# Weights of three later layers prepared in slices during the first layer and kept in DRAM

## The chip, the core and the metric

The kernel runs on one core of a Trainium2 chip. The metric is the device time of one execution in microseconds (us). All data are 32-bit floats. The engines are called as in the profile: PE (TensorE, matrix products; PEld is its loading of the stationary operand), DVE (VectorE), ACT (ScalarE), POOL (GpSimd) and SP (SyncE, which here issues nearly all DMAs). SBUF is the on-chip memory of 128 partitions, PSUM the eight banks into which PE writes, DRAM the memory off the core.

## What is computed

The input x has 128 batch elements of 128 nodes by 512 features, and adj one 128 x 128 matrix for each element. Four graph layers follow one another, and each ends with `x = layernorm(x + layer(x, adj))`:

- Layer 0: a transition matrix T is made from adj and from scores of the nodes; the result is `relu(x Wk0 + T x Wk1 + T T x Wk2 + biases)`.
- Layer 1: two hypergraph convolutions. The first multiplies by w1 (1024 x 512, used transposed), a layer norm with gamma and beta follows, the second multiplies by w2 (512 x 1024, transposed).
- Layer 2: an attention by scores `x w a`, then a product with w (512 x 512).
- Layer 3: eight-headed attention with wq, wk, wv and wo (512 x 512 each, transposed).

Before a layer can run, its weights must be brought into the form that its products read: w1, w2, wq, wk, wv and wo have to be transposed, gamma is multiplied into w2, and some vectors (beta through w2, bv through wo, w times a) are worked out.

## The kernel before

**Tiling.** Two batch elements make a pair (U = 2). There are n = 64 pairs, and one group of work is two pairs; each layer thus has 32 groups. The functions `layer0` (line 894), `layer1` (1007) and `layer23` (1168, layers 2 and 3 together) write down one group's work. Between layers x goes through DRAM (`x1d`, `x2d`).

**Products by Strassen's scheme.** `strassen` (565) makes a product of two 2 x 2 block matrices by seven products, with the weight blocks B11, B21, T1, B22, T2, T3 and N4, where T1 = B12 - B11, T2 = B22 - T1, T3 = B22 - B12 and N4 = B21 - T2 (`combine`, 493). `twice` (761) does this on two levels: seven outer products in the order B11, B21, T2, T1, B22, T3, N4, each of them a `strassen` of seven: 49 products on 49 inner blocks. The weights of layer 0, w1 and the pair wq with wk are used by `twice`; w2, w, wv and wo by one level.

**Preparation.** `load_T` (500) loads 128 rows of a weight at a time, transposes each 128 x 128 part on PE against an identity matrix into PSUM (`ident`), copies it to SBUF on ACT and at the end subtracts blocks on DVE. With `by_blocks` it first regroups the columns on DVE. `prepare1` (972) does this for w1 and w2, `prepare2` (1122) for wq and wk, `prepare_w` (1143) for w, `prepare3` (1152) for wv and wo. All tiles of the program are written under line 369 of the profile, since `emit` (358) issues every instruction.

**Order of the work.** Nothing is issued where it is written. `Plan.add` (186) records every operation with a key, and `Plan.order` (232) then simulates the five engines with estimated durations and gives the order of the instructions of each engine. PE takes the ready instruction with the lowest key; the other engines go by deadlines that `deadlines` (347) finds backwards from PE's starts. An SP transfer without anything to wait for is held until PE has reached its key. A key counts pairs: layer 0 runs over keys 0 to 64, layer 1 from 65, layers 2 and 3 from 130.5. The preparations have keys of their own, in lines 1341 to 1352:

```python
for job, start, step in ((prepare1, n - 5, .5),):
...
for job, start, step in ((prepare2, 2 * n + LAG1 - .3, .1), (prepare_w, 2 * n + LAG1, 0),
                         (prepare3, 2 * n + LAG1 + 2, .1)):
```

So w1 and w2 are prepared from five pairs before the end of layer 0, and the other weights where layer 1 ends.

**Memory.** The planner also gives out SBUF. A tile is of a kind, and a kind has a number of places. The general kind is "four" (1024 floats a partition), with 12 places at first (BUFS). Each group of layer 0 writes its results into two tiles of kind "out" (3088 floats), of which there are four (OUTS). One large tensor, `first`, holds the seven weight blocks of layer 0 ("w7", 2702 floats each); later the same memory holds, for layer 1, the additional inner blocks of w1 ("q3") and tiles "h" for layer 1's hidden rows, and then, for layers 2 and 3, the blocks of wq and wk ("q7", 1792 floats each). Behind it lies "w28", the seven blocks of w2. A place becomes free when all that lay there before is done with (`later`, line 400 on). When the "out" tiles, w28, the tile `rows1` and the tiles `ks` are done with, their memory becomes further "four" places. In layer 1 the blocks of w1 lie in seven "four" tiles and seven "q3".

Of the kernel before, what the change touches and what calls it, by code (L numbers as in the profile page):

```python
# [32 lines left out]
OUTS = 4  # L33
# [10 lines left out]
SOFT = .2  # L44
RAMP = 0, 0, .05, 4
# [20 lines left out]
SIZE = {"four": U * D, "sq": U * (P + 2), "bank": D, "col": 12, "row": D, "w28": 7168, "q7": 7 * 2 * P, "q3": 3 * 2 * P, "h": U * D,  # L66
        "w7": 7 * QW, "out": U * 4 * QW, "t0": D, "t1": D, "row1": 4 * D, "k": U * (P + 2)}

PSUM = "bank", "t0", "t1"


class Tile:
# [3 lines left out]
    def __init__(self, kind, ap=None):  # L76
        self.kind, self.ap = kind, ap
        self.reads, self.writes = [], []
# [88 lines left out]
class Plan:  # L167


    def __init__(self, slots, later):  # L170
        self.slots = slots
        self.later = later
        self.key = 0
        self.group = None
        self.share = 1
        self.ops = []
# [9 lines left out]
    def add(self, engine, call, name, args, kw):  # L186
# [13 lines left out]
        else:  # L200
            k = len(self.ops)
            op = [engine, [(call, args, kw)], ns, (self.key, k), set(), [], shares_port(engine, name, args, kw), moved]
# [29 lines left out]
    def order(self, urgent=None):  # L232
# [40 lines left out]
        def look(e):  # L273
# [3 lines left out]
            for k, t in ready[e].items():  # L277
                if e == SP and ops[k][3][0] > reached and not ops[k][4]:
                    continue
# [24 lines left out]
        while count < n:  # L304
# [4 lines left out]
            for tile in o[5]:  # L309
                if tile not in place:  # L310
                    s, l = slots[tile.kind], line[tile.kind]
                    at = min(s)
# [10 lines left out]
            if e == PE and o[3][0] > reached:  # L323
                reached = o[3][0]
                stale.add(SP)
# [52 lines left out]
def kernel(  # L378
# [19 lines left out]
    spans = {"w7": (7, 0), "q3": (7, 0), "h": (7, 7 * SIZE["q3"]), "q7": (7, 0), "w28": (1, 7 * SIZE["q7"])}  # L398
    at = lambda kind, k: spans[kind][1] + k * SIZE[kind]
    for kind, (n, _) in spans.items():  # L400
        places[kind] = [first[:, at(kind, k):at(kind, k) + SIZE[kind]] for k in range(n)]
        if kind != "w7":
            for k in range(n):
                later[kind, k] = [(old, i) for old in (("q3", "h") if kind == "q7" else ("w7",))
                                  for i in range(spans[old][0])
                                  if at(old, i) < at(kind, k) + SIZE[kind] and at(kind, k) < at(old, i) + SIZE[old]]
    slots = {"w7": 7, "out": OUTS, "q7": 0, "q3": 0, "h": 0, "w28": 0, "sq": SQS, "col": COLS, "row": ROWS, "bank": 6, "t0": 1, "t1": 1,
             "four": BUFS, "row1": 1, "k": KS}
# [6 lines left out]
    places["row1"] = [const.tile([P, SIZE["row1"]], FP, name="rows1")]  # L415
    ks = const.tile([P, KS * SIZE["k"]], FP, name="ks")
    places["k"] = [ks[:, k * SIZE["k"]:(k + 1) * SIZE["k"]] for k in range(KS)]
    later["four", len(places["four"])] = [("k", k) for k in range(KS)]
    places["four"].append(ks[:, :SIZE["four"]])
    for kind, k, t in (*(("out", k, t) for k, t in enumerate(outs)), ("w28", 0, places["w28"][0]),  # L420
                       ("row1", 0, places["row1"][0])):
# [7 lines left out]
    def tile_of(kind, *shape):  # L429
        n = math.prod(shape)  # L430
        flat = View(Tile(kind), np.arange(SIZE[kind]))[:, :n]
# [46 lines left out]
    class Split:  # L478


        def __init__(self, block, more):
            h = block.shape[2] // 2
            self.parts = {B11: block[:, 0, :h], B21: block[:, 1, :h], B12: block[:, 0, h:], B22: block[:, 1, h:],
                          T2: more[:, 0], T3: more[:, 1], N4: more[:, 2]}

        def __getitem__(self, key):
            return self.parts[key[1]]

# [11 lines left out]
    def load_T(W, srcs, nk, nh, with_stage=None, by_blocks=False, scale=1.0, twice=False):  # L500


        n = 0
        for src in srcs:
            for o in range(src.shape[0] // P):
                st = four().rearrange("p u f -> p (u f)")[:, :src.shape[1]]
                sp.dma_start(st, src[o * P:(o + 1) * P])
                if with_stage:
                    with_stage(o, st)
                half, at = divmod(n, nh)  # L510
                if by_blocks:
                    by = four().rearrange("p u f -> p (u f)")[:, :src.shape[1]]
                    ve.tensor_copy(by.rearrange("p (c k a) -> p k c a", k=4, a=Q),
                                   st.rearrange("p (k c a) -> p k c a", k=4, a=Q))
                    st = by
                st = st.rearrange("p (c n) -> p c n", n=P)
                for g in range(src.shape[1] // D):
                    pt = bank()
                    with plan.together():
                        for c in range(C):  # L520
                            pe.transpose(pt[:, c * P:(c + 1) * P], st[:, g * C + c], ident)
                    pt = pt.rearrange("p (c n) -> p c n", n=P)
                    for c0 in range(0, C, nk):
                        kk = (g * C + c0) // nk
                        blk = ((B11, B21), (B12, B22))[half][kk]
                        m = min(nk, C)
                        k0 = (g * C + c0) % nk
                        if twice:
                            q = at // (nh // 2)
                            to = W[blk][:, 2 * q:2 * q + 2, 0, at % (nh // 2):at % (nh // 2) + P]  # L530
                        else:
                            to = W[:, blk, k0:k0 + m, at:at + P]
# [851 lines left out]
```

## Time and profile before

Three runs took 5474.72, 5475.79 and 5477.9 us; the profiled execution's span is 5473.7 us.

| | |
|---|---|
| layer 0, end of a group to the next | 39.7 us |
| layer 1, the same | 55.1 us |
| layers 2 and 3, the same | 71.4 us |
| DMA, whole span | 768.35 MB, mean 140 GB/s |
| source loads of w1 and w2 | issued from 1222 to 1374 us |
| source loads of w, wq, wk, wv, wo | issued from 3066 to 3189 us |
| last product with layer 0's weights | starts at 1332 us |
| first product with w1 | starts at 1333.5 us |

The distances of the groups are those of the DMA issues that write x1d, x2d and the output. An answer of the trace on a stretch of time gives, for each engine, the time that it was busy and the number of its instructions, then the clock that PE was granted (1.00 is full), the busy share of the 16 DMA engines and what they moved. A table of waits says which engine stood idle until which other engine's instruction had ended. A line of the timeline has the start, the duration, the engine, the operation, the tile written and those read, and how many equal instructions were merged.

### The profile page before, as it was taken

The numbers are of one execution on the slowest core, as the hardware profiler recorded it, in microseconds if no ns is written. First come the engines' busy times: TensorE is split into PE (matmuls) and PEld (weight loads), VectorE is DVE, ScalarE is ACT, GpSimd is POOL, SyncE is SP. The second block draws the span as 40 slices with busy tenths as digits, with TensorE's granted clock in tenths as the row PEclk, the third lists the DMA queues.
The fourth block names the chain that finished last, engine by engine and source line by source line (L and its number), as shares of the span: only waits on it lengthen the run. The fifth ranks groups of instructions, "written<-read, shape, count | busy, mean of one in ns | idle before, by whom it ended". The sixth has DMA issues, their size and how long they took to land.

```text
span 5473.7 us, 94041 instructions
## 1 busy us (share of the span) xinstructions
PE 5349.7 (98%) x29145; PEld 4259.2 (78%) x29145; DVE 4551.0 (83%) x11561; ACT 2392.4 (44%) x6471; POOL 4041.0 (74%) x4835
## 2 busy tenths in 40 slices
PE   8999999999999999999999999999999999999998
PEld 4555555555788888888888789999999999999987
DVE  6788888878998899998889978778878777878876
ACT  2444343434434434443434344444455445445444
POOL 6666666666777777877777567777777777777776
PEclk8999999999999999999999999999999999999999
DMA  3333333334454545545445545554555554555553
GB/s 93 104 98 98 101 101 102 94 103 129 145 150 144 155 144 148 155 148 152 147 148 150 161 129 165 161 162 154 162 162 156 162 163 151 162 166 159 160 154 119
DMA packets 788381, 768.35 MB, mean 140 GB/s; under 512 B 264859, under 2 KB 592547, under 8 KB 787878
## 3 DMA queue, kind: packets, MB, share of 16 engines
q1 hardware_dynamic: 786374, 759.71, 45.8%
q8 instruction: 231, 3.78, 0.3%
q10 hardware_dynamic: 1504, 2.62, 0.2%
q14 instruction: 272, 2.23, 0.1%
HBM read 435.83 MB, written 326.24 MB: 139 GB/s over the span
## 4 chain that ended last, share of the span: by engine, by line
PE 57%; DVE 7%; DMA 3%; POOL 1%; issue 1%; ACT 1%; SPq 1%; DVEq 0%; POOLq 0%; ACTq 0%
PE bank L369 43%; PE t L369 15%; DVE first L369 2%; DVE col L369 2%; DVE out L369 1%; DVE four L369 1%; SPq L369 1%; POOL out L369 1%; DMA h<-first 1%; DMA out<-h 1%; ACT first L369 0%; DVE junk L369 0%; DMA first<-x3d 0%; POOL first L369 0%; POOL four L369 0%
## 5 line engine op out<-in xcount | busy, mean ns | idle before, releaser
L369 PE MATMUL bank<-first,four 128*128 128x386 f32 (+3 forms) x5176 | 1437.1, 431 | 37.2 <-DVE out L369 14.8
L369 PEld LDWEIGHTS bank<-first,four 128*128 128x128 f32 (+2 forms) x5176 | 847.7, 187 | 592.9 <-DVE out L369 139.0
L369 DVE TENSOR_TENSOR out<-bank,out 128x386 f32<-128x386 f32 (+1 forms) x1884 | 928.1, 510 | 282.4 <-PE bank L369 223.3
L369 POOL TENSOR_TENSOR out<-out 128x256 f32<-128x256 f32 (+3 forms) x482 | 550.4, 1152 | 300.6 <-DVE out L369 210.0
L369 POOL TENSOR_TENSOR col<-col,neghalf 128x1 f32<-128x1 f32 x640 | 380.6, 600 | 377.8 <-DVE col L369 376.2
L369 DVE TENSOR_TENSOR first<-bank,first 128x256 f32<-128x256 f32 x1362 | 543.6, 414 | 130.2 <-PE bank L369 100.6
L369 PE MATMUL bank<-first,out 128*128 128x256 f32 (+2 forms) x2560 | 624.0, 382 | 26.4 <-DVE first L369 9.4
L369 PEld LDWEIGHTS bank<-first,out 128*128 128x128 f32 (+1 forms) x2560 | 469.2, 190 | 128.7 <-DVE first L369 30.8
L369 PE MATMUL bank<-four,out 128*128 128x256 f32 (+2 forms) x2118 | 538.4, 376 | 2.2 <-DVE col L369 1.4
L369 DVE TENSOR_TENSOR four<-bank,four 128x256 f32<-128x256 f32 x818 | 338.4, 418 | 142.1 <-PE bank L369 127.5
L369 PE MATMUL bank<-out,first 128*128 128x128 f32 (+2 forms) x2840 | 427.9, 290 | 0.9 <-DVE out L369 0.4
L369 ACT COPY out<-bank 128x258 f32<-128x258 f32 (+2 forms) x555 | 236.7, 431 | 436.8 <-PE bank L369 388.6
L369 PEld LDWEIGHTS bank<-four,out 128*128 128x128 f32 (+2 forms) x2118 | 369.8, 189 | 58.5 <-issue 8.4
L369 PEld LDWEIGHTS bank<-out,first 128*128 128x128 f32 (+1 forms) x2840 | 374.5, 188 | 24.7 <-DVE four L369 2.8
L369 ACT ACTIVATE col<-col,col 128x1 f32<-128x1 f32 x640 | 183.2, 292 | 456.4 <-POOL col L369 388.2
L369 POOL TENSOR_TENSOR four<-four,four 128x256 f32<-128x256 f32 (+2 forms) x395 | 328.8, 837 | 14.4 <-DVE col L369 4.8
L369 ACT COPY t<-out 128x512 f32<-128x512 f32 x256 | 150.2, 591 | 421.1 <-DVE four L369 248.8
L369 POOL TENSOR_TENSOR first<-first 128x512 f32<-128x512 f32 (+3 forms) x196 | 234.4, 1208 | 105.5 <-DVE first L369 67.4
L369 POOL TENSOR_TENSOR four<-four 128x256 f32<-128x256 f32 (+2 forms) x331 | 245.4, 758 | 66.9 <-DVE four L369 36.3
L369 POOL TENSOR_TENSOR out<-out,out 128x256 f32<-128x256 f32 (+2 forms) x286 | 287.2, 1008 | 9.3 <-DVE four L369 4.5
L369 POOL TENSOR_SCALAR sq<-sq,col 128x128 f32<-128x128 f32 x256 | 160.7, 638 | 148.8 <-DVE col L369 146.5
L369 DVE BATCH_NORM_STATS2 col<-first 128x6 f32<-128x512 f32 x370 | 245.7, 681 | 26.9 <-ACT first L369 25.1
(407 smaller groups left out, 12718.5 us busy)
## 6 DMA issues: line engine op xcount, KB each, us to landing
h<-first SPq DMA_DIRECT2D x496, 128.0 KB, 2.4
out<-x1d SPq DMA_DIRECT2D x88, 512.0 KB, 4.5
out<-h SPq DMA_DIRECT2D x87, 512.0 KB, 4.6
four<-in_x_dram SPq DMA_DIRECT2D x512, 64.0 KB, 2.0
four<-in_x_dram SPq DMA_DIRECT2D x62, 512.0 KB, 3.6
x1d<-four SPq DMA_DIRECT2D x62, 512.0 KB, 2.7
first<-S SPq DMA_DIRECT2D x61, 512.0 KB, 4.4
out<-S SPq DMA_DIRECT2D x50, 512.0 KB, 4.4
```

The costliest lines, as they stand in the source:

```text
L369: call(*map(real, args), **{n: real(a) for n, a in kw.items()})
```

## The change

1. **Preparation in slices.** `load_T`, `Split` and the four `prepare` functions go. For each weight there is now a `park_` function, a generator that makes the final blocks slice by slice (a slice is 128 columns of the block, s = 0 and 1) in tiles of a new kind "prep", and writes every piece to a DRAM tensor (`Parked.keep`). w1 and the pair wq, wk are kept with all inner blocks (`park_49`), w2, w, wv and wo with seven blocks.
2. **Transposing.** w1 and wo are transposed on PE as before. w2, wq, wk and wv are loaded by four DMAs for each 128 rows that already exchange the 32 x 32 blocks (`exchanged`), and DVE transposes within the blocks (`turned`, `turned_part`). gamma is multiplied in on POOL after the transposition.
3. **Loading.** `take_49`, `take_w2` and `take_halves` load the kept blocks at the changes of layer, one DMA for each outer block.
4. **Keys.** All parking runs from key 3 in steps of 0.95 (54 steps); its operations rank 4 keys later (`late`), but their transfers are let go by the unshifted key.
5. **Memory.** OUTS is 3 and not 4. The memory goes to `side`, three tiles "prep", which later become "four". Three more "prep" lie in `ks` and `rows1`, which layer 1 needs only later. "q3" and "h" go: w1's 49 inner blocks lie in seven "q7", and the hidden rows of layer 1 in "four". The seven "w7" have fixed places in the order of use.
6. **Reading w1.** An inner block of w1 is now read as two runs of 128 columns, 896 apart (`Laid`).

The diff, cut to its core:

```diff
-OUTS = 4
+OUTS = 3
+SPACE = 3
...
+PARKED, LATE = .95, 4
...
-            op = [engine, [(call, args, kw)], ns, (self.key, k), ..., moved]
+            op = [engine, [(call, args, kw)], ns, (self.key + self.late, k), ..., moved, self.key]
...
-                if e == SP and ops[k][3][0] > reached and not ops[k][4]:
+                if e == SP and ops[k][8] > reached and not ops[k][4]:
...
-    spans = {"w7": (7, 0), "q3": (7, 0), "h": (7, 7 * SIZE["q3"]), "q7": (7, 0), "w28": (1, 7 * SIZE["q7"])}
+    spans = {"w7": (7, 0), "q7": (7, 0), "w28": (1, 7 * SIZE["q7"])}
...
+    side = const.tile([P, SPACE * SIZE["prep"]], FP, name="side")
+    places["prep"] = [ks[:, :SIZE["prep"]], *(t[:, k * SIZE["prep"]:(k + 1) * SIZE["prep"]]
+                                              for t, n in ((row1, 2), (side, SPACE)) for k in range(n))]
...
+    def exchanged(t, src):
+        for k in range(4):
+            sp.dma_start(t[k * Q:(k + 1) * Q].rearrange("p (m w) -> p m w", m=4), src.rearrange("(m r) (k w) -> k r m w", r=Q, k=4)[k],
+                         run=src.shape[1] // 4, parts=Q)
...
+    def park_49(to, source):
+        for s in range(2):
+            As = [prep().rearrange("p (b g i e) -> p b g i e", b=2, g=2, i=2) for _ in range(2)]
+            yield from source(s, As)
+            Bs = [prep().rearrange("p (t g i e) -> p t g i e", t=2, g=2, i=2) for _ in range(2)]
+            c11, c21, c12, c22 = (A[:, b] for b in range(2) for A in As)
+            (t1, t2), (t3, n4) = [[B[:, t] for t in range(2)] for B in Bs]
+            po.tensor_tensor(t1, c12, c11, OP.subtract)
+            ve.tensor_tensor(t3, c22, c12, OP.subtract)
+            po.tensor_tensor(t2, c22, t1, OP.subtract)
+            ve.tensor_tensor(n4, c21, t2, OP.subtract)
+            at = lambda k, i, m, s=s: lambda t: t[:, s, 2 * k:2 * k + 2, i * P:(i + m) * P]
+            for k, M in enumerate((*As, *Bs)):
+                to.keep(at(k, B11, 2), M[:, :, 0].rearrange("p b i e -> p b (i e)"), run=2 * P)
+                to.keep(at(k, B22, 1), M[:, :, 1, 1], run=P)
+            yield
+            for k, M in enumerate((*As, *Bs)):
+                N = prep().rearrange("p (j t e) -> p j t e", j=2, t=4)
...
+                on = (ve, po)[k % 2]
+                on.tensor_tensor(t1, b12, b11, OP.subtract)
...
+                to.keep(at(k, T1, 1), t1, run=P)
+                to.keep(at(k, T2, 3), N[:, :, 1:].rearrange("p j t e -> p j (t e)"), run=3 * P)
+                yield
...
+    def take_49(name):
+        tiles = [tile_of("q7", 2, 7, P) for _ in range(7)]
+        WT[name] = [Laid(t) for t in tiles]
+        for j in (B11, B21, T2, T1, B22, T3, N4):
+            k = (B11, B12, B21, B22, T1, T2, T3, N4).index(j) if j != T1 else 4
+            PARK[name].take(tiles[j].rearrange("p s i e -> p s (i e)"), lambda d, k=k: d[:, :, k], run=7 * P)
+            yield
...
-        h = [[tile_of("h" if i0 + 2 * U < B else "four", U, D) for _ in range(U)] for _ in range(2)]
+        h = [[four() for _ in range(U)] for _ in range(2)]
...
-    for job, start, step in ((prepare1, n - 5, .5),):
...
+    plan.late = LATE
+    spaced(3, PARKED, park_w1(), park_w2(), park_vectors(), park_qk(), park_w(), park_v(), park_o())
+    plan.late = 0
+    spaced(n - 1.5, .1, take_49("w1"), take_w2())
     layer(layer1, n + LAG1, WHEN1, size=2)
...
+    spaced(2 * n + LAG1 - 1, .1, take_halves("w"))
+    spaced(2 * n + LAG1, .1, take_49("qk"))
+    spaced(2 * n + LAG1 + 2, .1, take_halves("v", "o"))
     layer(layer23, 2 * n + LAG1 + LAG2, WHEN2, ramp, size=2)
```

## The prediction

> **What bounds the kernel now.** I read the page's busy line first, then the chain that ended last, then the busy time by stage, then both changes of layer in slices of 20 us.
>
> ```profile
> PE 5349.7 (98%) x29145; PEld 4259.2 (78%) x29145; DVE 4551.0 (83%) x11561; ACT 2392.4 (44%) x6471; POOL 4041.0 (74%) x4835
> PE 57%; DVE 7%; DMA 3%; POOL 1%; issue 1%; ACT 1%; SPq 1%; DVEq 0%; POOLq 0%; ACTq 0%
> ```
>
> TensorE carries the chain. The table by stage (length, then busy us and instructions of PE, PEld, DVE, ACT, POOL, then granted clock, DMA share, GB/s) shows where it does not:
>
> ```profile
> 120.00:1220.00 1100.00, 1095.39 (x3258) 590.44 (x3257) 898.29 (x2302) 455.97 (x1062) 739.58 (x886) 1.00 0.34 100
> 1220.00:1300.00 80.00, 73.18 (x223) 36.93 (x221) 56.81 (x145) 30.21 (x73) 44.20 (x55) 1.00 0.36 103
> 1300.00:1440.00 140.00, 123.71 (x537) 90.63 (x538) 131.64 (x326) 54.57 (x112) 104.47 (x130) 0.95 0.47 139
> 1440.00:3080.00 1640.00, 1611.26 (x7673) 1354.62 (x7673) 1481.13 (x3662) 668.93 (x1255) 1273.61 (x1481) 1.00 0.50 149
> 3080.00:3280.00 200.00, 180.46 (x1071) 153.48 (x1070) 167.69 (x401) 79.90 (x236) 112.23 (x137) 0.97 0.47 144
> 3280.00:5400.00 2120.00, 2114.04 (x15711) 1931.48 (x15711) 1691.67 (x4466) 1042.99 (x3551) 1645.48 (x2023) 1.00 0.51 159
> ```
>
> PE idles 4.6 us in 1100 of layer 0 and 6 in 2120 of layers 2 and 3, but 6.8 + 16.3 = 23.1 us at the first change and 19.5 at the second. There its clock falls too:
>
> ```profile
> 1380.00:1400.00 20.00, 14.51 (x58) 11.14 (x58) 19.87 (x43) 10.02 (x15) 8.39 (x9) 0.74 0.38 95
> 1400.00:1420.00 20.00, 15.72 (x68) 12.01 (x68) 19.51 (x51) 6.79 (x12) 14.31 (x17) 0.91 0.68 200
> 3120.00:3140.00 20.00, 14.86 (x54) 11.01 (x53) 19.75 (x33) 5.20 (x12) 7.71 (x7) 0.83 0.37 101
> 3200.00:3220.00 20.00, 16.19 (x93) 14.87 (x91) 17.99 (x39) 1.70 (x4) 15.00 (x20) 0.83 0.33 90
> ```
>
> Busy time by the missing share of clock is 14.5 x 0.26 + 15.7 x 0.09 = 5.2 us at the first change and (14.9 + 16.2) x 0.17 = 5.3 at the second. In three of the four slices DVE is full, and the waits of PE in 1300 to 1440 (us, times, longest) name it:
>
> ```profile
> PE bank L369 <- DVE first L369: 6.5, 6, 3.4
> PE t L369 <- ACT first L369: 3.0, 3, 2.1
> ```
>
> So **28.3 us are lost at the first change and 24.8 at the second**, beside the preparation's own PE work.
>
> **What the Trainium skill says.** "Perfetto Trace Analysis", section Identifying the Most-Contended Engine, warns that matmul busy time is a bad measure of headroom. The trace agrees: layer 0 is 99.6% busy on PE with 53.7% on PEld. So I use idle time, not busy time, as what can be won. "TensorE: Matmul & The Clock Gate", Part 1, says that an idle PE falls to a lower clock and needs sustained work to come back; the trace agrees, 0.74 in the slice that holds the 3.4 us wait. "SBUF — State Buffer", Who interferes with whom, says that a VectorE instruction with two SBUF inputs and a GpSimd one block each other for a whole instruction. The trace fits: the 1024-wide tensor_tensor of DVE at the first change takes 1220 ns in one group and 1580 in another.
>
> **The change, part by part.**
>
> *PE transposes.* prepare1, prepare2 and prepare3 transpose 8 + 8 + 8 + 4 + 4 blocks of 128x512, four transposes each: 128. The new code keeps them for w1 and wo alone (48, now in layer 0); w2, wq, wk and wv are crossed by DMA and DVE. Price of one, from the timeline:
>
> ```profile
> 1264.08 0.60 PE L369 MATMUL bank<-ident,four 128*128 128x128 f32 x4
> ```
>
> Four take 0.60 us with the pipeline's end of 0.272 (the duration of one), so each adds (0.60 - 0.27) / 3 = 0.11. 80 go: **-8.7 us**. The 48 that stay cost 5.2 us on PE before and after. The few of the vectors move likewise.
>
> *First change.* Out of 1220 to 1440 go the loads, 16 PSUM copies on ACT, and on DVE the dots with beta (8 x 0.88 = 7), the products with gamma (about 4 x 1.4 = 6), the regrouping copies (4.9), the outer combinations (two of four, 8 x 1.2 = 10) and 16 of the 28 small inner ones (16 x 0.41 = 7, the rest on POOL): some 34 us of DVE. In 1300 to 1440 DVE is busy 131.6 of 140; without most of this it stands near layer 1's own level. The inner combinations also sat between the last product of layer 0 and the first of layer 1, since q3 lies under layer 0's weights. And the seven "four" tiles of w1, taken out of twelve while layer 0 ends, return: 5 become 15 with the side tiles. Of 28.3 us I keep what layer 1 has anyway (28.7 idle in 1640, so 4 in 220) and 2 for new waits: **-22 us**, bounds -10 (half of the DVE waits were the fill of the pipeline) and -28.
>
> *Second change.* Out go 10.1 us of DVE for the 1792-wide combinations, 8.0 for sixteen inner ones, 4.9 of copies, some 5 of dots, 3 to 4 for w: about 31 us, again where DVE is full (3080 to 3140). But from 3140 to 3220 PE loses 7.5 us with DVE mostly not full, which looks like layer 2's own start. I take half of 24.8: **-12 us**, bounds 0 and -25.
>
> *Added to layer 0.* From the code, with durations of equal shapes (DVE 1024-wide 1.21, 512-wide 0.67, 256-wide 0.41, transposes 1.23 and 0.43, dot 0.76; POOL 0.73 and 1.28; 1024-wide 2.4, scaled from 1823 ns for 772): w1 11 on DVE and 22 on POOL; wq and wk 18 and 22; w2 15 and 10; w, wv, wo and vectors 19 and 5; in all **63 us DVE, 58 POOL**, 10 ACT. Spread over 54 steps of 0.95 in key, behind layer 0's own work by 4 in key, they lift DVE from 81.7% of 1100 us to 87.4% and POOL from 67.2% to 72.5%. What hides them is the free time of these engines; what may not hide is the blocking of single instructions. Bounds: nothing, or the idle share of layer 1, where DVE stands at 90.3%: 1.75% of 1100 = 19, less the 4.6 there now, 15 us. I take **+4**.
>
> *SP and DMA.* About 216 DMAs join SP's queue in layer 0, 7 a group of 39.7 us, at 0.4 us of issue each 2.8 us beside some 40 x 0.43 = 17 now. A slice kept in DRAM waits on SP for its subtraction, and behind it stand loads of x and of adj (asked for three keys, some 60 us, ahead) and the crossing of e, which has no such lead. That is within the +4. Kept 23.9 MB and 12 MB read add 30 GB/s to 100 at a share of 0.34: hidden.
>
> *Loads at the changes.* w1 comes back as 7 x 0.92 MB, w2 as 3.7; wq and wk as 6.4, w 1.8, wv and wo 3.7. A 20 us slice of the trace carried 274 GB/s at a share of 0.82, so about 334 full (estimate); beside a share of 0.5, 167 GB/s are left and a tile lands in 5.5 us. Tile k needs only the one or two layer 0 blocks under it, and with places given in the order of use these end one product (5.5 us) apart. The first comes free near 1296, the first product of layer 1 stands at 1333. Hidden, 0 to +20 us a change; I take 0 beyond the 2 above. "DMA: Bandwidth & Descriptors", Bandwidth, gives 341 GB/s for 1 MB, close to the 334.
>
> *OUTS 4 to 3.* The new group's second result tile can be written only when the old group's first is done with. Already now it is so:
>
> ```profile
> 802.78 1.02 PE L369 MATMUL t<-out,sq 128*128 128x512 f32 x2
> 804.29 1.02 PE L369 MATMUL t<-out,sq 128*128 128x512 f32 x2
> 806.33 0.55 DVE L369 TENSOR_TENSOR out<-bank,out 128x386 f32<-128x386 f32 x1
> ```
>
> The last read by the transition product ends at 805.3, the first write to the next tile is at 806.3, and the groups that I followed through layer 0 keep that order. So three tiles are used now: 0, bounds 0 and 1 us for each of 32 groups.
>
> *Strided weights.* w1 is read as two runs of 128. The 512-wide product over four runs of 128 takes 595 ns and the contiguous one 592: 0. *"h" joins "four"*: layer 1 has 24 tiles either way, but in one pool; its order is planned anew, 0, bounds -8 and +8.
>
> Sum: -8.7 - 22 - 12 + 4 = -38.7, on the span of 5473.7: 5435.0. The three runs stand 1 to 4 us above that span, the median 2.1: **5437 us**.
>
> **The rivals.** *Waits are replaced* (0.11): the fill of layers 1 and 2 or late weight tiles cost what DVE did; only the transposes and some 5 us of memory pressure are won, less 4 in layer 0: 5475.8 - 9.7 = 5466. For it: PE's losses after 3140 without a full DVE, and 10 and 12 MB at the changes. Against: the named waits and room on the DMA queues. *Layer 0 is disturbed, slower* (0.11): each of the 54 steps puts long POOL and DVE instructions ahead of a result that PE waits for, in a stage where PE idles 0.4%. The longest, 2.4 us on POOL, can hold the shared port against DVE. At 1.5 us a step this is 81 us against 42.7 won: 5514. It decides from 42.7 / 54 = 0.8 us a step. Against it: DVE has 18% free and six PSUM banks stand between it and PE. *The change doesn't do what it says*: the planner puts slices late, into layer 1 (DVE 90%); the keys end at 58 of 64, so little chance (0.02, near 5470). The forecast has 0.76.
>
> **How the numbers follow.** Within the forecast the terms reach from -8.7 - 28 - 25 - 8 = -70 (5406) to -8.7 - 10 + 15 + 8 = +4 (5480). With a tenth of the chance of the slow rival beyond it, and a little below 5406, the range is 5405 to 5479. A change under 0.2% (11 us) can't be told from none: faster is below 5465, slower above 5487. Of the forecast's 0.76 some 0.03 lies within it, and of the replaced waits' 0.11 some 0.03 is still faster: faster 0.76, same 0.13, slower 0.11.
>
> **What would show it.** Right: PE idle at each change under 10 to 14 us with the clock back near 1.00; no transposes of weights there but the vectors'; DVE near 87% in layer 0 with PE idle under 9 us in 1100; no PE wait that ends with a load of a kept slice. Wrong: groups of layer 0 longer than 39.7 us; PE waiting for "first" tiles that a DMA from DRAM writes; losses after 3140 unchanged.

## The result, and the profile after

The changed kernel takes **5456.67 us**, median of four runs (5451.87 to 5463.22), beside 5475.26 of four runs of the kernel before. The ratio is 0.9965 with a 95% interval of 0.995 to 0.9979. It is faster, and inside the range, but it wins 18.6 us where 38.7 were forecast. The profiled execution's span is 5461.4 us, 12.3 less than the span of before; this execution is the slowest of the four. The accounts by stage below are made on these two.

The page's busy line and its chain first:

```profile
PE 5338.6 (98%) x29065; PEld 4256.9 (78%) x29065; DVE 4544.2 (83%) x11573; ACT 2382.0 (44%) x6437; POOL 4032.8 (74%) x4875
PE 76%; DVE 10%; DMA 4%; POOL 3%; SPq 3%; issue 2%; ACT 1%; DVEq 0%; POOLq 0%; ACTq 0%
```

PE has 80 instructions less, as worked out, and is 11.1 us less busy. Its idle time, the span less the busy time, was 124.0 us and is 122.8: taken together it has been moved and not taken away. Where it went, the table by stage shows (length, busy us and instructions of PE, PEld, DVE, ACT, POOL, clock, DMA share, GB/s):

```profile
120.00:1220.00 1100.00, 1081.60 (x3237) 585.35 (x3236) 947.47 (x2365) 447.74 (x1048) 782.16 (x916) 1.00 0.45 131
1440.00:3080.00 1640.00, 1614.06 (x7691) 1366.55 (x7690) 1476.23 (x3663) 678.49 (x1257) 1229.67 (x1485) 1.00 0.51 153
3080.00:3280.00 200.00, 190.46 (x1189) 165.69 (x1189) 152.85 (x394) 74.96 (x214) 125.08 (x156) 1.00 0.52 163
3280.00:5400.00 2120.00, 2108.78 (x15609) 1920.04 (x15608) 1683.23 (x4439) 1032.51 (x3568) 1637.39 (x2007) 1.00 0.51 157
```

The idle time of PE in 3080 to 3280 has fallen from 19.5 to 9.5 us and its clock is back at 1.00. In layer 0 it has risen from 4.6 to 18.4 us. DVE and POOL are busy there just as forecast (947 of 1100 is 86.1%, 782 is 71.1%), and DMA too (131 GB/s). So the work added was estimated well, and its effect on PE was not.

The first change of layer comes some 25 us later than before, so the same stretch is not at the same clock time. Moved by 25 us it is this:

```profile
1245.00:1465.00 220.00, 205.72 (x791) 135.93 (x791) 172.50 (x475) 89.71 (x185) 145.46 (x186) 0.99 0.55 171
```

PE idles 14.3 us in these 220 against 23.1 before, and DVE has 16 us less to do. Of the four slices shown before, the two at the second change read now:

```profile
3120.00:3140.00 20.00, 19.11 (x94) 15.69 (x93) 10.52 (x22) 4.20 (x10) 10.15 (x12) 1.00 0.76 254
3200.00:3220.00 20.00, 16.09 (x117) 13.80 (x116) 15.41 (x42) 11.89 (x47) 7.43 (x10) 1.00 0.41 116
```

Where DVE was full from 3120 on, it is half idle, PE waits little, and the clock holds at 1.00. From 3200 on PE idles 3.9 us of 20, as before, but at full clock. (This change comes some 11 us later than before, so the slices do not hold quite the same work.) Which wait has grown in layer 0 is told by PE's table of waits in 120 to 1220 (us, times, longest); first before, then after:

```profile
PE bank L369 <- DVE out L369: 2.6, 5, 1.0
```

```profile
PE bank L373 <- DVE out L373: 11.3, 12, 1.9
PE bank L373 <- ACT out L373: 2.0, 5, 0.7
PE t L373 <- POOL col L373: 1.7, 1, 1.7
```

PE wants a PSUM bank, and the bank is full because DVE has not yet added it into an "out" tile. In five of these twelve waits, 7.0 of the 11.3 us, DVE was at instructions of the slices until just before. They are known by their tiles `rows`, `side` and `ks`, which DVE does not touch in layer 0 of the kernel before. This is one of the five (start, duration, engine, operation, tile written and read):

```profile
1002.99 1.95 POOL L373 TENSOR_TENSOR out<-out 128x772 f32<-128x772 f32 x1 [1.07 <-DVE out L373]
1003.18 2.03 DVE L373 TENSOR_TENSOR rows<-side 128x256 f32<-128x256 f32 x1
1005.14 0.55 DVE L373 TENSOR_TENSOR out<-bank,out 128x386 f32<-128x386 f32 x1
1005.74 0.59 PE L373 MATMUL bank<-first,four 128*128 128x386 f32 x1 [1.54 <-DVE out L373]
```

The slice's subtraction takes 2.03 us, where 26 others of its shape in this stage take 0.41 on average; an instruction of POOL runs beside it that began before it. The addition that frees the bank stands behind it on DVE.

**An account by stage.** Layers do not begin at the same time in two kernels, so I mark the end of a piece of work and not a clock time: the DMA issues (counted from 1) that write x1d for the 3rd and 57th time, x2d for the 3rd and 55th, the output for the 3rd and 59th, and the end. Between them lie the start, layer 0, the first change (with the last four groups of layer 0), layer 1, the second change, layers 2 and 3, and the end. Each entry is the stage's length less that of the kernel before, in us, from one profiled execution each; the last column is the ratio of the timed runs to those of the kernel before beside them. That kernel itself took between 5474.4 and 5482.9 us in the five comparisons, so kernels of different comparisons are set against one another by their ratios; 0.001 of it is 5.5 us. A single write is a rough mark: in the changed kernel the 53rd to 59th writes of x1d come between 29.1 and 37.4 us later than before, so a difference of a few us between two entries means little.

| kernel | start | layer 0 | 1st change | layer 1 | 2nd change | layers 2, 3 | end | sum | ratio |
|---|---|---|---|---|---|---|---|---|---|
| after | 3.2 | 25.9 | -4.9 | -13.2 | -23.2 | 0.9 | -0.9 | -12.3 | 0.9965 |
| e2 no writes of slices | 5.1 | 22.6 | -14.6 | -15.7 | -22.3 | 4.6 | 0.3 | -20.1 | 0.9952 |
| e4 no arithmetic | 4.0 | 20.1 | -9.6 | -9.2 | -31.1 | 11.1 | -0.2 | -15.0 | 0.9972 |
| e3 no slices, 3 outs | 7.8 | 36.7 | -5.8 | -11.8 | -20.9 | 0.6 | -0.9 | 5.7 | 1.001 |
| e8 no slices, 4 outs | 5.4 | -3.4 | -25.5 | -25.3 | -25.9 | -3.8 | 0.5 | -77.8 | 0.9859 |
| e5 before, 3 outs | -1.7 | 8.3 | 7.8 | -9.8 | 4.5 | 5.0 | 0.2 | 14.3 | 1.0033 |
| e6 after, 4 outs, 9 fours | 5.0 | 28.9 | -15.4 | -23.9 | -23.6 | -0.2 | -0.9 | -30.0 | 0.9941 |
| e7 after, 4 outs, 11 fours | 12.1 | 11.4 | -17.3 | -21.5 | -21.9 | 3.6 | -0.4 | -34.1 | 0.9946 |
| e9 after, T asked earlier | -5.2 | 45.9 | -7.0 | -16.8 | -34.4 | 8.5 | -0.2 | -9.2 | 0.9979 |
| e10 e7 without arithmetic | 8.6 | 19.7 | -11.5 | -33.0 | -24.7 | -2.1 | 0.8 | -42.2 | 0.9915 |
| e11 e7 without writes | 11.7 | 21.1 | -24.6 | -12.3 | -22.2 | 5.1 | -1.2 | -22.5 | 0.9949 |
| e12 e7, later start | 9.6 | 7.1 | -26.0 | -20.9 | -25.5 | -1.3 | 2.5 | -54.6 | 0.9882 |
| e13 after, later start | 5.2 | 17.3 | -11.3 | -13.0 | -21.1 | 3.3 | -0.6 | -20.3 | 0.9946 |

The first row is the result in short: **the second change wins 23 us and layer 1 13, the first change only 5, and 29 are lost at the start and in layer 0.** A group of layer 0 takes 40.71 us and not 39.67 (mean of 26 groups).

### The profile page after: what moved, and what is told of

It reads as the page before. It is cut to its first block, busy times and chain, and to the rows that moved or that the text cites. A ratio compares the mean times of both kernels' runs of the same rounds, so it can differ in the third digit from the quotient of the medians.

```text
span 5461.4 us, 93897 instructions
## 1 busy us (share of the span) xinstructions
PE 5338.6 (98%) x29065; PEld 4256.9 (78%) x29065; DVE 4544.2 (83%) x11573; ACT 2382.0 (44%) x6437; POOL 4032.8 (74%) x4875
## 4 chain that ended last, share of the span: by engine, by line
PE 76%; DVE 10%; DMA 4%; POOL 3%; SPq 3%; issue 2%; ACT 1%; DVEq 0%; POOLq 0%; ACTq 0%
PE bank L373 58%; PE t L373 19%; DVE out L373 3%; DVE four L373 3%; SPq L373 3%; DVE col L373 2%; POOL four L373 1%; DVE side L373 1%; DMA sq<-in_adj_dram 1%; POOL out L373 1%; DMA first<-x3d 1%; DMA four<-in_x_dram 0%; DMA out<-x3d 0%; ACT out L373 0%; DVE sq L373 0%
## 5 line engine op out<-in xcount | busy, mean ns | idle before, releaser
L373 PE MATMUL bank<-first,four 128*128 128x386 f32 (+3 forms) x6114 | 1733.2, 430 | 58.4 <-DVE out L373 21.8
L373 PEld LDWEIGHTS bank<-first,four 128*128 128x128 f32 (+2 forms) x6114 | 1070.3, 189 | 640.1 <-DVE out L373 132.1
L373 POOL TENSOR_TENSOR out<-out 128x772 f32<-128x772 f32 (+3 forms) x250 | 350.2, 1408 | 263.2 <-DVE out L373 189.4
L373 PEld LDWEIGHTS bank<-first,out 128*128 128x128 f32 (+2 forms) x2048 | 372.3, 189 | 77.3 <-issue 9.5
L373 PE MATMUL bank<-first 128*128 128x128 f32 (+1 forms) x2356 | 329.6, 278 | 1.9 <-DVE four L373 1.3
L373 ACT ACTIVATE four<-four,col,col 128x512 f32<-128x512 f32 (+1 forms) x367 | 324.2, 887 | 7.4
L373 PEld LDWEIGHTS bank<-first 128*128 128x128 f32 (+1 forms) x2356 | 300.5, 189 | 18.1 <-issue 2.9
L373 DVE BATCH_NORM_STATS2 col<-four 128x6 f32<-128x512 f32 x430 | 287.6, 678 | 4.8 <-ACT four L373 3.1
L373 PE MATMUL t<-out,sq 128*128 128x512 f32 x512 | 255.5, 594 | 6.4 <-DVE sq L373 2.5
L373 PE MATMUL bank<-four,first 128*128 128x256 f32 (+3 forms) x1424 | 253.3, 322 | 2.7 <-DVE first L373 1.1
```

Source lines behind the costliest of these rows:

```text
L373: call(*map(real, args), **{n: real(a) for n, a in kw.items()})
```

## The experiments

Two theories stood against each other at first: that the slices themselves disturb layer 0 (by their writes through SP and DMA, or by their arithmetic on DVE and POOL), and that the third "out" tile, which the prediction had put at nothing, costs the time.

**Leaving out the slices or a part of them (e2, e3, e4).** e2 leaves out the DMAs that write the pieces to DRAM, but for one small write to each tensor; the loads at the changes read x in their place, in the same amounts:

```diff
-            sp.dma_start(part(self.tile, how, self.kept), src, run=run)
-            self.kept += 1
...
-            sp.dma_start(dst, part(self.tile, how, 0, self.kept), run=run)
+            sp.dma_start(dst, part(self.tile, lambda t: how(self.x), 0, self.kept), run=run)
```

> The changed kernel without the writing of slices to DRAM: all slices are still loaded, transposed and subtracted, but not kept, and layers 1 to 3 load the same number of bytes in the same shapes from x in the place of their weights. If SP's queue or the DMA engines hold up layer 0 (theory: kept slices stand ahead of the crossing of e), its group falls to about 39.9 us and the time to some 20 us below the changed kernel. If the arithmetic on DVE and POOL does it, the group stays above 40.4 us and the time within 8 us of the changed kernel.

Ratio 0.9952 (0.9935 to 0.9968), 5453.88 us. The interval overlaps that of the change; layer 0 loses 22.6 and not 25.9. The writes are not shown to cost anything.

e3 leaves out the transposing and subtracting of the slices as well, still with three "out" tiles. Beside its own work layer 0 then has only the loads and dot products for the vectors (sixteen on DVE, 16.0 us):

```diff
-        for s in range(2):
-            As = [prep().rearrange("p (b g i e) -> p b g i e", b=2, g=2, i=2) for _ in range(2)]
...
+        to.keep(None, None, P)
+        yield
```

> The changed kernel without any slice: nothing of the seven blocks is loaded, transposed, subtracted or kept, only the vectors are prepared, and layers 1 to 3 load the same bytes from x in the place of their weights. OUTS is 3. If the slices as a whole cost layer 0 its 1.0 us a group, the group is back at 39.7 us and the time is some 30 us below the changed kernel (about 5427). If three result tiles cost it, the group stays near 40.5 us. Beside that this run gives what the changes of layer cost without slices: about the same idle time as in the changed kernel is expected.

Ratio 1.001 (1.0003 to 1.0016), 5483.52 us: with almost nothing of the slices left to disturb it, the kernel is **slower than with them**, by some 25 us (0.0045). PE's waits in 120 to 1220:

```profile
PE bank L373 <- ACT out L373: 26.5, 16, 1.8
PE bank L373 <- DVE out L373: 5.2, 9, 1.7
PE t L373 <- issue: 0.8, 1, 0.8
```

From the 14th group on the groups take 42.0 us each, and in each there is one wait of the first kind, 1.65 us on average. This stretch of the timeline (start, duration, engine, operation, tile written and read) shows one of them:

```profile
952.39 0.37 ACT L373 COPY out<-bank 128x258 f32<-128x258 f32 x1 [0.23 <-DVE out L373]
...
953.43 1.92 DVE L373 TENSOR_TENSOR out<-bank,out 128x386 f32<-128x386 f32 x4
...
955.23 1.88 PE L373 MATMUL t<-out,sq 128*128 128x512 f32 x4
```

As I read it (the profile leaves out the numbers of the tiles), the copy and the additions belong to the new group, and the transition products at 955.2, which read the first tile of the old group, come only after them and end at 957.1. The new group's second tile is written from 958.3 on. With three tiles the old group's first must be done with by then; the two groups are tied to one another.

e4 keeps the loads, the transpositions and the writes, but leaves out all subtractions and the product with gamma:

```diff
-            po.tensor_tensor(t1, c12, c11, OP.subtract)
-            ve.tensor_tensor(t3, c22, c12, OP.subtract)
-            po.tensor_tensor(t2, c22, t1, OP.subtract)
-            ve.tensor_tensor(n4, c21, t2, OP.subtract)
...
-                po.tensor_tensor(A, A, gammas[:, :, None].to_broadcast([P, CH, P]), OP.mult)
```

> The changed kernel with every slice loaded, transposed and kept, but without the subtractions and the product with gamma: the parts that would be subtracted are kept in the place of the differences (34 us of DVE and 58 us of POOL go). If the arithmetic on DVE and POOL holds up layer 0, its group falls to 39.9 us and the time to some 20 us below the changed kernel. If SP's queue or the DMA engines do it, the group stays above 40.4 us.

Ratio 0.9972 (0.996 to 0.9983), 5461.3 us, no faster than the change. DVE falls from 947 to 910 us in layer 0, POOL from 782 to 730, and layer 0 still loses 20.1 us. So neither half of the slices' work is shown to explain the loss alone, and with three tiles even its absence does not give it back.

**Three tiles in the kernel before (e5).** The kernel before with three tiles and nothing else (e1) gave no result, so no run changes the tile alone. In e5 the memory of the fourth is given to three more "four" places:

```diff
-BUFS = 12
+BUFS = 15
...
-OUTS = 4
+OUTS = 3
```

> The kernel before with three result tiles, their memory given to the general tiles from the start (OUTS = 3, BUFS = 15), nothing else. The run without any slice still had groups of 41.1 us in layer 0, so the slices can't be what costs layer 0 its time. If three result tiles are the cause by themselves, layer 0's group here takes 40.5 us or more and layer 0 ends some 30 us later than in the kernel before; the end of layer 0 may win back up to 10 us by the additional general tiles, so that the time is 10 to 35 us above the kernel before. If something else in the changed kernel is the cause (fixed places, the other tiles), the group stays at 39.7 us and the time at or below the kernel before.

Ratio 1.0033 (1.0019 to 1.0047), 5493.85 us: **18 us slower** than the kernel before in the same comparison (5475.71). A group takes 40.05 us and not 39.67. So the third tile is not free even in the kernel from whose trace the prediction had read that it is. Layer 1 wins 9.8 us here though it has no more room than before: each "out" tile becomes three "four" places once layer 0 is done with it, so from then on both kernels have the same number. The gain seems to lie in the new order.

**Four tiles in the changed kernel (e6, e7, e8), and another order with three (e9).** e6 takes the memory from "four":

```diff
-BUFS = 12
+BUFS = 9
...
-OUTS = 3
+OUTS = 4
```

> The changed kernel with four result tiles, paid for by three general tiles in layer 0 (OUTS = 4, BUFS = 9). If the third result tile is what layer 0 lacks, its group falls from 40.7 to about 39.9 us and the time to some 20 us below the changed kernel (about 5437). If nine general tiles are too few for layer 0, the group stays above 40.4 us and this run alone can't tell.

e7 takes it from the "prep" tiles instead and from one "four"; with less room `park_49` works off one inner block after another:

```diff
-BUFS = 12
+BUFS = 11
...
-OUTS = 3
-SPACE = 3
+OUTS = 4
+SPACE = 1
...
-            for k, M in enumerate((*As, *Bs)):
+            inner(2, B)
+            yield
+            B = prep().rearrange("p (t g i e) -> p t g i e", t=2, g=2, i=2)
...
+            inner(3, B)
+            yield
```

> The changed kernel with four result tiles, one side tile and eleven general tiles; the slices of w1, wq and wk are worked through one block after the other, so that four tiles of kind prep are enough. Same work, same writes. By the theory of the result tiles the group of layer 0 is 39.7 to 39.9 us, layer 0 ends about where it does in the kernel before, and the time is 5425 to 5440. By the theory that slices disturb layer 0, the group stays above 40.3 us and the time within 8 us of the changed kernel.

e6 has 0.9941 (0.9927 to 0.9956) and e7 0.9946 (0.9931 to 0.9961), 5442.79 and 5444.06 us: 10 to 13 us faster than the change by the ratios, with intervals that still overlap its own. In e6 none of this is in layer 0, where nine "four" tiles seem to cost as much as the fourth "out" gives; it is in the first change and in layer 1. In e7 start and layer 0 lose 23.5 us and not 29.1.

e8 is e7 with the slices left out as in e3:

```diff
-BUFS = 12
+BUFS = 11
...
-OUTS = 3
-SPACE = 3
+OUTS = 4
+SPACE = 1
```

> The run without any slice, with four result tiles, one side tile and eleven general tiles (weights of layers 1 to 3 are read from x as there). The earlier run without slices had groups of 41.1 us with three result tiles. If the result tiles are the cause, the group is 39.7 us here, and the time some 45 us below that run, at 5425 to 5440. Against the run with slices and four result tiles it gives the price of the slices in layer 0: 4 us by my prediction, 0 to 15 by its bounds.

Ratio 0.9859 (0.9842 to 0.9875), **5397.52 us**, some 83 us (0.0151) below e3. Its waits of PE in layer 0 are near those of the kernel before again:

```profile
PE bank L373 <- DVE out L373: 2.5, 7, 0.6
PE t L373 <- ACT t L373: 2.3, 2, 1.5
PE bank L373 <- ACT out L373: 0.8, 2, 0.4
```

Between the profiled executions of e3 and e8 42.5 us lie in the start and layer 0, 19.7 in the first change and 21.5 behind it, where both have the same work and the same number of places.

The ratios make a small table:

| | three "out" tiles | four |
|---|---|---|
| slices left out | 1.001 (e3) | 0.9859 (e8) |
| slices done | 0.9965 (after) | 0.9946 (e7) |
| kernel before | 1.0033 (e5) | 1 |

Going from four tiles to three costs 10 (after against e7), 18 or 83 us. Three more pairs follow from the runs below: 2 without the writes (e2 against e11), 31 without the arithmetic (e4, e10) and 35 with a later start (e13, e12). All six have the same sign, though in two of them (10 and 2) the intervals overlap. So three tiles have a price, but no single one; in e3 the order falls into a cycle that is not seen in the change. What is shown is the price of the exchange: the fourth tile's memory comes from "prep" and "four" tiles, and each exchange gives a new order. The slices cost 47 us with four tiles (5444.06 less 5397.52, of one comparison), of which 21.5 lie in the start and layer 0 and the rest in later stages, whose work is the same. Both effects belong to layer 0's term of the prediction or to "OUTS"; together they had been put at 4.

That the fourth tile is put to use by the slices can be counted. For 25 groups of layer 0 I took the end of the old group's transition products on its first tile, and the first 386-wide addition of the new group after its four additions of biases, which is a good stand-in for the first write to its second tile. If that write stands ahead of the old tile's last read, four tiles are in use:

| kernel | tiles | groups of 25 with the write ahead | median of write less last read, us |
|---|---|---|---|
| before | 4 | 0 | 1.2 |
| after | 3 | 1 (by 0.1) | 1.2 |
| e8, no slices | 4 | 3 | 1.5 |
| e10, no arithmetic | 4 | 9 | 0.7 |
| e7 | 4 | 16 | -2.2 |
| e12 | 4 | 19 | -3.5 |
| e11, no writes | 4 | 21 | -2.4 |
| e6 | 4 | 25 | -12.0 |

The count errs by some groups: in e9 below, with three tiles, it gives 3 (down to -4.8 us), where there should be none, so the 3 of e8 can't be told from none.

Before, the order never needed the fourth tile in these groups, as the prediction had read, but it kept clear of it by 1.2 us only. My reading is that slices delay the transition now and then by more than that, and then a fourth tile lets the new group go on, where with three it stops. This reading does not reach e3 and e8: there hardly a group uses the fourth tile, and three tiles cost the most.

e9 tries to have the transition done earlier, with three tiles, by smaller keys:

```diff
-WHENT = (.8, 2.1), (2.0, 3.1)
+WHENT = (.6, 2.1), (1.75, 3.1)
```

> The changed kernel, three result tiles, with the transition of a group's first pair planned earlier (keys .6 and 1.75 in the place of .8 and 2.0), so that its result tile is done with before the next group asks for it. If the cost is that the next group's second result tile waits for this transition, the group falls to about 39.9 us and the time to some 20 us below the changed kernel. If three tiles are too few whatever the order, the group stays above 40.4 us.

Ratio 0.9979 (0.9971 to 0.9987), 5461.21 us, no better than the change, and layer 0 loses 45.9. A key alone does not undo it.

**What the slices cost with four tiles (e10, e11, e12).** e10 is e7 without the arithmetic (as e4), e11 e7 without the writes (as e2):

```diff
-                on.tensor_tensor(t1, b12, b11, OP.subtract)
-                on.tensor_tensor(t2, b22, t1, OP.subtract)
...
-                po.tensor_tensor(A, A, gammas[:, :, None].to_broadcast([P, CH, P]), OP.mult)
```

> The run with slices, four result tiles and eleven general tiles (5444 us), without the subtractions and the product with gamma; slices are loaded, transposed and kept as there, with undifferenced parts in the place of the differences. With slices the fifty-seventh write of x1d stands 23.5 us later than in the kernel before, without any slice 2.0. If DVE and POOL carry that price, it falls to about 10 us here (5 of them transposes on PE) and the time to some 5430. If SP's queue and the DMA engines carry it, it stays at 20 or more and the time within 8 us of 5444.

```diff
-            sp.dma_start(part(self.tile, how, self.kept), src, run=run)
-            self.kept += 1
```

> The run with slices, four result tiles and eleven general tiles (5444 us), without the writes of slices to DRAM; they are loaded, transposed and subtracted as there, and layers 1 to 3 load the same bytes from x. If SP's queue and the DMA engines carry the price of the slices, the write of x1d stands about 10 us later than in the kernel before (23.5 with the writes) and the time is some 5430. If DVE and POOL carry it, it stays at 20 or more and the time within 8 us of 5444.

e10 has 0.9915 (0.9898 to 0.9931), 5435.19 us; e11 0.9949 (0.9934 to 0.9964), 5454.59. By the ratios the arithmetic is worth some 17 us of the 47, with intervals that just touch, and the writes nothing. Neither in e10 nor in e11 is layer 0 better than in e7 (19.7 and 21.1 against 11.4); what e10 wins, it wins in layer 1 and behind it (11.5 and 7.3 us). PE's idle time in 120 to 1220 falls from 18.4 to 11.7 us without the arithmetic with three tiles (e4), which is near the 7.0 us of waits behind slices, but rises from 13.6 to 17.4 with four (e10). So neither half of the slices' work is shown to carry the 47 us alone.

e12 is e7 with the slices begun later and set closer:

```diff
-    spaced(3, PARKED, park_w1(), park_w2(), park_vectors(), park_qk(), park_w(), park_v(), park_o())
+    spaced(8, .85, park_w1(), park_w2(), park_vectors(), park_qk(), park_w(), park_v(), park_o())
```

> The run with slices, four result tiles and eleven general tiles (5444 us), with the slices begun at key 8 in steps of 0.85 in the place of key 3 in steps of 0.95. With slices from key 3 the third write of x1d stands at 154.5 us, without slices at 147.9. If the first slices hold up the start of layer 0, that write comes back to about 148 and the time falls by some 6 us, to 5438. If the price of the slices is spread evenly over layer 0, the time stays within 4 us.

Ratio **0.9882 (0.9867 to 0.9897), 5417.7 us**. It computes everything and beats both kernels: 65 us below the kernel before of the same comparison (5482.91), and by the ratios some 35 below e7 and 45 below the change. In the profiled executions it is 20.5 below e7: start and layer 0 win 6.8, the first change 8.7 and the rest 5.

e13 makes the same edit in the kernel as changed, with three tiles:

```diff
-    spaced(3, PARKED, park_w1(), park_w2(), park_vectors(), park_qk(), park_w(), park_v(), park_o())
+    spaced(8, .85, park_w1(), park_w2(), park_vectors(), park_qk(), park_w(), park_v(), park_o())
```

> The change as made, with one edit: the preparation in layer 0 begins at key 8 in steps of 0.85 and not at key 3 in steps of 0.95 (54 steps, both end by key 54), so the first groups of layer 0 run without it. Theory (the start of the slices costs by itself, whatever the number of result tiles): the gain of the run with four result tiles and the same start, 26 us against its own base, comes back nearly whole, 5430 to 5440, with the shift of start and layer 0 together down from 29 to 15 or less. Rival (the gain came from a new order of the whole plan that four result tiles allowed): 5450 to 5462, start and layer 0 together still 25 or more, and no part of the gain where the edit is.

Ratio 0.9946 (0.9932 to 0.996), 5449.0 us. Neither expectation holds: the span is 8 us below that of the change, the ratio 0.0019 below it (10 us), and start and layer 0 together lose 22.5 where the first theory wanted 15 or less and the rival 25 or more. The later start is worth something with three tiles, as it seems (the intervals overlap), and more with four. The rows of the table by stage for 120 to 1220, e7 first and e12 second, don't show where e12 has it from:

```profile
120.00:1220.00 1100.00, 1086.38 (x3264) 590.14 (x3263) 958.86 (x2383) 453.08 (x1055) 787.86 (x924) 1.00 0.45 132
```

```profile
120.00:1220.00 1100.00, 1088.17 (x3269) 590.55 (x3268) 968.27 (x2394) 450.78 (x1064) 787.52 (x926) 1.00 0.46 132
```

PE is 1.8 us busier, with DVE 9.4 us busier too. I found no single wait that went; the gain lies in small amounts in four stages, in an order that was planned anew.

## Why the prediction was right or wrong

**Right in sign and place at the changes of layer.** PE's transposes went (80 instructions fewer), DVE is no longer full (78% of the 220 us at the first change, 76% of the 200 at the second), and the clock is at 0.99 and 1.00. This is what "TensorE: Matmul & The Clock Gate", Part 1, of the Trainium skill leads one to expect once PE idles less, and the trace agrees. *Second change*: half of the 13.9 for all 128 transposes (8.7 and 5.2) and 12 for DVE make -19; measured -23.2. *First change*: the same half and 22 make -29. PE's idle time fell by 8.8 us in the stretch moved by 25, but the stage as marked won only 4.9. With four tiles and otherwise the same work it won 15.4 (e6), 17.3 (e7) and 26.0 (e12), and in all five pairs made from the changed kernel the one with four tiles wins more here, by 1.9 (e4, e10) to 19.7 us (e3, e8). So the mechanism was right as far as idle time and clock go, and with three tiles a part of the gain is missing. It is not missing in the last groups of layer 0: from PE's first product of the 29th group to its last with layer 0's weights there were 177.0 us before, and there are 168.5 in the change and 168.0 in e7. From there to the third write of x2d it is 176.0, 179.3 and 170.9; the two part at the start of layer 1, and why is open.

**Where it failed: "OUTS 4 to 3 ... So three tiles are used now: 0".** The order was read rightly, and the runs confirm it (0 of 25 groups). What failed is the step from "the order does not need the tile" to "the tile is worth nothing". A margin of 1.0 us was there to be read in the three lines shown (805.3 to 806.3), and the same prediction put up to 2.4 us long instructions into the same stage. The loss is 18 us in the kernel before (e5), 10 to 13 in the changed one (e6, e7) and 2 to 83 in the other pairs. The bound that I had written, 32 us, held; the value chosen, 0, was its lower end.

**Where it was mis-sized: "Added to layer 0: +4".** Busy times were forecast well (DVE 86.1% for 87.4, POOL 71.1% for 72.5). The loss at the start and in layer 0 is 29.1 us. Of it, PE's own transposes are 8.0, from this list of PE's groups in 120 to 1220 (operation, tiles, count, busy us, mean ns):

```profile
L373 PE MATMUL bank<-ident,rows 128*128 128x128 f32 x16 | 2.4, 273 | 0.0
L373 PE MATMUL bank<-ident,side 128*128 128x128 f32 x16 | 2.2, 273 | 0.0
L373 PE MATMUL bank<-ident,ks 128*128 128x128 f32 x16 | 2.2, 273 | 0.0
L373 PE MATMUL bank<-ident,cols 128*128 128x128 f32 x8 | 1.2, 273 | 0.0
```

They are the 48 of w1 and wo and 8 of vectors (0.143 us each, where 0.11 had been taken), for which 5.2 had been allowed as moved. In the start and layer 0 as marked (0 to 142.5 to 1215.2 before, 0 to 145.7 to 1244.3 after) PE idles 17.0 us more and is busy 12.1 us more; beside the transposes that leaves 4 us of busy time that I cannot place. Less the 5.2, it is 24 us for a forecast of 4, bounds 0 and 15. With four tiles it is 18.3 (e7), with the later start 11.5 (e12): the upper bound, from the idle share of layer 1, was closer than the value taken.

**Rivals.** *Layer 0 is disturbed* has its mechanism for a part: slices stood ahead of what PE wanted in 7.0 of 11.3 us of waits for DVE. On average, the third tile's share included, it is 24 / 54 = 0.44 us a step, with four tiles 18.3 / 54 = 0.34, where 0.8 was the point; the same steps begun later come to 11.5 / 54 = 0.21 (e12), so this is no fixed price of a step. *Waits are replaced* at the changes did not come about: in the two stretches no wait of PE ends with a load of a kept block, though these land only 7.2 us (w1) and 7.3 (w2) after their issue, where 5.5 had been estimated for w1. Over the whole span, though, PE's idle time fell by 1.2 us only. *The change doesn't do what it says* did not come about: the slices are in layer 0.

**The signs named.** The clock, DVE's share in layer 0, the absence of waits for kept blocks and the losses after 3140 came out on the right side: PE idles 6.6 us from 3140 to 3220 and idled 10.3 before, which the prediction puts at 7.5. The first change, at 14.3 us of idle time, stands just outside its 14. PE's idle time in layer 0 (18.4 us, where under 9 was wanted) and the length of a group (40.7) were signs of being wrong, and both came.

**Small terms.** *"h" joins "four"* was put at 0, bounds -8 and 8; layer 1 won 13.2, outside, and e6, e7 and e12 won 21 to 24. That it is the one pool is not shown: e5 wins 9.8 there with the same number of places and the same work as before. *SP and DMA*: right. DVE waited 10.7 us for loads of x in layer 0 before, and 2.2 after. *Strided weights*: right, as the mean of w1's 256-wide product with "four" tiles is 382 ns after and 381 before.

By stage, then, the forecast was +9 (4 and the transposes moved), -29, 0, -19; the profiles show +29, -5, -13, -23. Two errors of 20 and 24 us to the bad and two of 13 and 4 to the good leave 12 us of gain in the profiled executions, and 18.6 in the timed runs. In part this is luck: the 13 us of layer 1, forecast as 0 and not explained, are as much as the whole gain of the profiled executions.

**What stays open.** Why the slices cost 47 us with four tiles, and why so much of it comes back with a later start, is not settled. Neither arithmetic nor writes carry it alone. Every edit makes `Plan.order` give the whole program a new order, and e3 and e12, and layer 1 in e5, suggest that such an order can be worth 10 to 20 us or more in either direction; that is my reading of them, and it was not isolated by a run that keeps the order and changes only the work.

## What to carry to other kernels

When memory is taken from a stage, look not only at whether its order needs the buffer, but by how many microseconds it does without it, and compare that with the longest instruction that the same change puts into the stage. Free time on the helping engines tells how much work fits in, not what PE waits: in a stage where PE is 99.6% busy, added work has to be priced by how it delays the next result that PE waits for (here, on average over 54 steps, between 0.2 and 0.44 us a step, by tiles and start). In a kernel whose order a planner makes, undo the parts of a change one by one, since a part that looks harmless, or the absence of work, can move the whole order.

## What the runs showed that I had not expected

Work taken away made the kernel slower: with three tiles the kernel without any slices has a ratio of 1.001 and with them 0.9965. An order can lock two groups into a cycle (42.0 us, each with one wait of about 1.7), which the kernel with slices doesn't show (40.71 on average).

Subtractions of equal shape in the slices differ widely on DVE in layer 0 of the changed kernel (count, busy us, mean ns):

```profile
L373 DVE TENSOR_TENSOR rows<-side 128x256 f32<-128x256 f32 x3 | 4.7, 1557 | 0.0
L373 DVE TENSOR_TENSOR side<-ks,side 128x256 f32<-128x256 f32 x4 | 1.7, 424 | 0.0
```

The one takes 3.7 times the other. "SBUF — State Buffer", Who interferes with whom, which the prediction used, offers a reason, a POOL instruction that holds the port, and the trace shows the holder. Of the 50 subtractions of this width in the slices on DVE, 26 took 0.41 us on average and 24 more than 0.45; 23 of these 24 ended 0.28 to 0.29 us after the end of a TENSOR_TENSOR of POOL that was already running when they began, as in the lines of the wait at 1005.74. The 63 us that I had added up from unstretched rows left this out: the 50 took 34.9 us, where at 0.41 each they would have taken 20.7 (estimate). Yet e10, which leaves these subtractions out, won nothing in layer 0.
